# Layer 1 attention of a two-layer graph network: when the group ends, the transferred sums and the special tiles fall

## The chip, the cores and the metric

The kernel runs on one core of a Trainium2 chip. A core has five engines with queues of their own: TensorE (PE, matrix products; PEld is its loading of weights), VectorE (DVE), ScalarE (ACT), GpSimd (POOL) and SyncE (SP, which here only issues DMA transfers), and 16 DMA engines that all queues share. The metric is the device time of one execution in microseconds. The kernel before takes 2959.15 us, the median of three runs (2958.06 to 2962.82).

## The reference

`x` is 4096 x 512 and `adj` a 4096 x 4096 matrix of zeros and ones. Two residual layers follow each other, each on `h = relu(layernorm(x))`. Layer 0 is a masked attention by `h @ edge_w`. Layer 1, which the change concerns, is a graph attention with 8 heads of 64 columns:

```python
data1 = (h @ W.T + b).reshape(N, H, D)                 # N 4096, H 8, D 64
src = einsum('nhd,xhd->nh', data1, src_proj);  trg = einsum('nhd,xhd->nh', data1, trg_proj)
e = src.T[:, :, None] + trg.T[:, None, :]              # head, target n, source m
e = where(e >= 0, e, 0.01 * e) + adj[None]             # the mask is added as 0 or 1
out = einsum('hnm,hmd->hnd', softmax(e, axis=-1), data1.transpose(1, 0, 2))
x = x + out
```

`adj` is added and excludes nothing, so every head needs all 4096 x 4096 weights. A weight is exp(adj) times the larger of two products of a row factor and a column factor, since the exponential of a leaky relu of a sum is such a maximum. No exponential per head and pair is needed, only exponentials of `adj`, shared by the heads, and one multiply-by-maximum per head.

## The kernel before, in words

Layer 0 and the linear part of layer 1 fill the first 1729 us; nothing in them is changed. Then comes the loop of layer 1's attention. It has eight **groups**: four blocks of `WL` = 1024 target rows, each for two sets of four heads. A group has 32 **steps**, one per tile `m` of 128 source rows. One list of 256 steps runs through all groups, and `stages` at its end calls each stage so many steps ahead; the order of these calls is the order of every engine's queue, written by hand:

- `load` (3 steps ahead) puts the transfer of a 128 x 1024 tile of transposed `adj` into SP's queue (tile `e`, three buffers). At certain `m` it also fetches for the next group the row factors `z` of four heads and the row `u`.
- `exps` (1 ahead) writes exp(adj) to PSUM (`ex`, one buffer) on ACT; `last_exps` (2 ahead, in `factors`) writes a scaled exponential `e3` for head 3 of the set; `relus` (2 ahead) prepares head 0.
- `weigh` (1 ahead) makes the four products `pr3, pr0, pr1, pr2`, in that order, on DVE (lines 846 and 849), each 128 x 1024. `pr0` has three buffers, the others two. At a **special tile** (`BY_LOG`), `pr0` comes from ACT instead: `logs`, five steps ahead, makes a relu on ACT and starts a transfer on POOL that adds the `adj` tile to it; ACT later takes its exponential (line 832). DVE then has three products.
- `gather` (0 ahead) multiplies the products on PE with the values, in column tiles of 32, so that four matmuls run beside each other (line 881), and sums denominators in a fifth PSUM bank `dn` (line 886).

The denominator of heads 1 and 2 goes through PE in each step. For head 3, POOL adds the products `pr3` into one tile (`acc3`, lines 856 and 858). For head 0 the products of most tiles (`BY_DMA`) are added up by transfers that accumulate, into two tiles `acc00` and `acc01` in turn (lines 863 and 865); the other tiles go through PE with a column of ones, as a pair of matmuls. `by_pe` and `side` in `gather` alternate which half of the four column groups such a pair occupies. The last step of a group multiplies the collected sums with the ones column, and head 3's last product as well. ACT copies the results out of PSUM (`os`, line 910).

The end of a group runs inside the next group's steps: `finish` is a generator, and one `next(ending, None)` per step takes one part of it. It copies the denominators (ACT, line 916), turns them (PE, line 920), takes reciprocals (DVE, line 924), turns each of eight output tiles (two transposes, line 936), scales it (four small ACT copies, line 960), adds two at a time to the residual by a transfer of POOL (line 963), and stores them through SP (line 966). The last group has `finish_last` instead. Group 0 has the generator `tables`, which prepares `z` and `u`.

All waits between engines are semaphores that follow from who reads and writes which tile. A buffer that is written again waits for its last reader, transfers included.

Of the kernel before, what the change touches and what calls it, by code (L numbers as in the profile page):

```python
# [8 lines left out]
FP = mybir.dt.float32  # L9
AF = mybir.ActivationFunctionType  # L10
ALU = mybir.AluOpType
# [4 lines left out]
P = 128  # L16
# [12 lines left out]
def kernel(  # L29
# [15 lines left out]
    nc = tc.nc  # L45
# [675 lines left out]

    HV = WL // BL
    JT = BL // P
    Q = P // 4
    BY_LOG = (17, 21, 25, 29)
    BY_DMA = [m for m in range(2, NT - 5) if m % 4 != 1]

    with tc.tile_pool(name="p", bufs=2) as prp, tc.tile_pool(name="rl", bufs=2) as rlp, tc.tile_pool(
        name="io1", bufs=3
    ) as iop, tc.tile_pool(name="s1", bufs=1) as sp, tc.tile_pool(name="za", bufs=1) as zp0, tc.tile_pool(name="e3", bufs=2) as e3p, tc.tile_pool(
        name="zb", bufs=1
    ) as zp1, tc.tile_pool(name="e", bufs=3) as ep, tc.tile_pool(name="ac", bufs=2) as acp, tc.tile_pool(
        name="os", bufs=1
    ) as osp, tc.tile_pool(name="u", bufs=1) as usp, tc.tile_pool(
        name="p_x", bufs=1, space=PSUM
# [11 lines left out]
        def tables():  # L750

            for h in range(H):
                nc.scalar.activation(s_n[:, h, :], s_n[:, h, :], AF.Relu, bias=tmb[:, h:h + 1])
                if h % 3 == 2:
                    yield
            pz = p_t.tile([P, 2, P], FP, name="pt")
            for g in range(H // HG):
                nc.tensor.transpose(pz[:NT, g, :], s_n[:, g * HG, :], ident)
            yield
            ut = sp.tile([NT, 2, P], FP, name="ut")  # L760
            nc.scalar.copy(ut, pz[:NT])
            nc.gpsimd.dma_start(u_d.rearrange("g t p -> t g p"), ut)
            nc.scalar.activation(s_n, s_n, AF.Exp, scale=-(1.0 - SLOPE))
            yield
            s_f = s_n.rearrange("p h t -> p (h t)")
            for c in range(H * NT // P):
                pz = p_t.tile([P, P], FP, name="pt")
                nc.tensor.transpose(pz, s_f[:, c * P:(c + 1) * P], ident)
                yield
                zt = sp.tile([P, P], FP, name="zt", bufs=2)  # L770
                nc.scalar.copy(zt, pz)
                nc.gpsimd.dma_start(z_d[c * P:(c + 1) * P, :], zt)
            yield
# [12 lines left out]
        def load(i, m):  # L786
            b, g = groups[i]
            e = ep.tile([P, WL], FP, name="e")
            nc.sync.dma_start(e, adj_t[m * P:(m + 1) * P, b * WL:(b + 1) * WL])
            ra[i, m] = e  # L790
            if i + 1 < len(groups) and m == 28:
                us[i + 1] = usp.tile([P, WL], FP, name="u")
                b, g = groups[i + 1]
                nc.sync.dma_start(us[i + 1], row_bcast(u_d, WL, g * N + b * WL))
            if i + 1 < len(groups) and m in (20, 22, 24, 26):
                zload(i + 1, ORDER[(m - 20) // 2])

        def scale(i, m):

# [17 lines left out]
            nc.scalar.activation(x_, ra[i, m], AF.Exp, bias=ld_m[:, h // HG, m:m + 1])  # L817
            e3[i, m] = x_

        def logs(i, m):  # L820
            if m in BY_LOG:
                b, g = groups[i]
                r = rlp.tile([P, WL], FP, name="lg", bufs=1)
                nc.scalar.activation(r, us[i], AF.Relu, bias=nlg_m[:, g, m:m + 1], scale=-(1.0 - SLOPE))
                nc.gpsimd.dma_start(r, adj_t[m * P:(m + 1) * P, b * WL:(b + 1) * WL], accum_op=ALU.add)
                rl[i, m] = r
# [11 lines left out]
        def weigh(i, m, order=ORDER):  # L838
            h = groups[i][1] * HG
            x_ = ex.pop((i, m))  # L840
            for k in order:
                if (i, m, k) in pr:
                    continue
                w = prp.tile([P, WL], FP, name=f"pr{k}", bufs=3 if k == 0 else 2)
                if k == 0:
                    nc.vector.scalar_tensor_tensor(w, rl.pop((i, m)), ngd_m[:, h // HG, m:m + 1], x_,  # L846
                                                   op0=ALU.subtract, op1=ALU.mult)
                else:
                    nc.vector.scalar_tensor_tensor(w, zs_[i, k], g_m[:, h + k, m:m + 1],  # L849
                                                   e3.pop((i, m)) if k == 3 else x_,  # L850
                                                   op0=ALU.max, op1=ALU.mult)
                pr[i, m, k] = w
            w = pr[i, m, 3]
            if m == 1:
                acc[i, 3] = acp.tile([P, WL], FP, name="acc3", bufs=1)
                nc.gpsimd.tensor_tensor(acc[i, 3], pr[i, 0, 3], w, ALU.add)
            elif 1 < m < NT - 1:
                nc.gpsimd.tensor_tensor(acc[i, 3], acc[i, 3], w, ALU.add)  # L858
            if m in BY_DMA:
                n = BY_DMA.index(m)  # L860
                if n < 2:
                    acc[i, 0, n] = acp.tile([P, WL], FP, name=f"acc0{n}", bufs=1)
                    nc.gpsimd.dma_start(acc[i, 0, n], pr[i, m, 0])
                else:
                    nc.gpsimd.dma_start(acc[i, 0, n % 2], pr[i, m, 0], accum_op=ALU.add)

        def gather(i, m):
            b, g = groups[i]
# [26 lines left out]
                    den(side * HV + q, zo[:, 1 - side:3], pr[i, m, 0], q, start=False, stop=False)  # L895
            if last:
                for q in range(HV):
                    den(HV + q, zo[:, 1:3], pr[i, m, 3], q, start=False, stop=False)
                for q in range(HV):
                    den(q, zo[:, 1:3], acc[i, 0, 1], q, start=False, stop=False)  # L900
                for r, a in enumerate((acc[i, 0, 0], acc[i, 3])):
                    for q in range(HV):
                        den(r * HV + q, zo[:, 1:3], a, q, start=False, stop=True)
# [9 lines left out]
        def denominators(i):  # L913
            os_, dn = late.pop(i)
            od = osp.tile([P, BL], FP, name="od")
            nc.scalar.copy(od, dn)
            yield os_
            pd = p_t.tile([P, JT, 2, 4], FP, name="pt")
            for j in range(JT):
                nc.tensor.matmul(pd[:, j, :, :].rearrange("p e r -> p (e r)"), od[:, j * P:(j + 1) * P],  # L920
                                 pick.rearrange("p e r -> p (e r)"), start=True, stop=True)
            yield
            rd = sp.tile([P, JT, 2, 4], FP, name="rd")
            nc.vector.reciprocal(rd, pd)
            yield rd

# [18 lines left out]
        def finish(i):  # L945


            dens = denominators(i)
            os_ = next(dens)
            yield  # L950
            next(dens)
            yield
            rd = next(dens)
            pts, os2 = {}, {}
            for t in range(WT + 4):
                if 0 < t <= WT:
                    if t % 2:
                        o = iop.tile([P, 2, HG, D], FP, name="o")
                    for r, k in enumerate(ORDER):
                        nc.scalar.activation(o[:, (t - 1) % 2, k, :], pts[t - 1][:, r, :], AF.Copy,  # L960
                                             scale=share(rd, t - 1, r))
                    if t % 2 == 0:
                        nc.gpsimd.dma_start(o, part(x1, i, t - 2, 2), accum_op=ALU.add)
                        os2[t] = o
                if t - 3 in os2:
                    nc.sync.dma_start(part(out, i, t - 5, 2), os2[t - 3])
                if t < WT:
                    pts[t] = p_t.tile([P, HG, D], FP, name="pt")
                    turn(os_, t, pts[t])
                yield  # L970

        def finish_last(i):

# [5 lines left out]
            os_ = next(dens)  # L979
            pts = [p_v.tile([P, HG, D], FP, name=f"pv{c}{q}") for q in range(HV) for c in range(2)]  # L980
            xs = p_x.tile([P, 4, HG, D], FP, name="ex")
            pts += [xs[:, n, :, :] for n in range(4)]
            for t in range(4):
                turn(os_, t, pts[t])
            next(dens)
# [28 lines left out]
        for k in ORDER:  # L1014
            zs_[0, k] = zp0.tile([P, WL], FP, name=f"z{k}")
            nc.sync.dma_start(zs_[0, k], row_bcast(s_d, WL, k * WL))
        load(0, 1)
        load(0, 2)
        first_e = ra[0, 0]
        exps(0, 0)  # L1020
        ra[0, 0] = first_e
# [28 lines left out]
        factors(0, 1)  # L1050
        scale(0, 1)

        stages = ((load, 3), (logs, 5), (exps, 1), (weigh, 1), (factors, 2), (scale, 2), (gather, 0))
        for s in range(len(steps)):
            for f, ahead in stages:
                if s + ahead < len(steps):
                    f(*steps[s + ahead])
            if s == 0:
                ending = tables()
            elif s % NT == 0:  # L1060
                ending = finish(s // NT - 1)
            if s == len(steps) - 2:
                ending = finish_last(len(groups) - 1)
            next(ending, None)
        for _ in ending:
            pass

# [33 lines left out]
```

## Time and profile before

| what | us |
|---|---|
| median of three runs | 2959.15 (2958.06 to 2962.82) |
| the profiled execution, its own time | 2957.07 |
| its span, first to last instruction | 2955.3 |
| the attention loop, from its first line 881 | 1729.4 on |
| group 0, with the loop's start | 155.25 |
| groups 1, 2, 3 | 150.74, 151.04, 152.38 |
| groups 4, 5, 6 | 150.21, 152.10, 150.22 |
| group 7, to the first transpose of the tail | 151.99 |

The profiled execution has 1.8 us outside its span. A group is measured from PE's first line 881 in it to that of the next group. PE's granted clock is 0.995 of full speed. In the attention loop the engines show 151.3 us (PE), 148.8 (DVE), 119.7 (ACT) and 94.8 (POOL) of busy time per group; the DMA engines have a mean share of 0.77 to 0.85. Products on DVE overlap: each is shown with 1.27 us, while their starts lie 1.19 us apart.

### The profile page before, as it was taken

Reading aid. Unit: us, or ns where it says so; the run is one execution under the profiler, and the core shown is the slowest. Engines: PE = TensorE matmul, PEld = TensorE weight load, DVE = VectorE, ACT = ScalarE, POOL = GpSimd, SP = SyncE. Lnnn points to the kernel's source line nnn. Section 1 sums busy time; section 2 is a strip of 40 time slices with the busy share of each in tenths; the row PEclk is TensorE's granted clock in tenths of the full one; section 3 lists DMA queues with packets and bytes.
Section 4 is the critical chain, followed back from the end, with each engine's and each line's share of the span. In section 5 each row is a group of like instructions: output and inputs, shape, how many; then the busy total and the mean of one; then the engine's idle time right before and its main releaser. Section 6 shows DMA issues by size and latency. Waiting matters only on the chain.

```text
span 2955.3 us, 42955 instructions
## 1 busy us (share of the span) xinstructions
PE 2911.4 (99%) x15179; PEld 1137.7 (38%) x15179; DVE 2534.6 (86%) x3584; ACT 1325.5 (45%) x1822; POOL 1380.0 (47%) x1043
## 2 busy tenths in 40 slices
PE   8999999999999999999999989999999999999998
PEld 4444444444444444444444423323222322232222
DVE  5435777778888998998996789999999999999998
ACT  2211111111121221221221068888777777777776
POOL 3401111113444444444444756565757575757574
PEclk9999999999999999999999999999999999999999
DMA  5525666667876766756653259696969696979795
GB/s 181 172 78 200 223 218 225 226 218 187 205 178 162 177 161 187 186 166 180 190 167 127 61 152 242 187 258 188 256 191 249 194 250 204 243 202 243 208 232 153
DMA packets 485160, 570.89 MB, mean 193 GB/s; under 512 B 265080, under 2 KB 315288, under 8 KB 484944
## 3 DMA queue, kind: packets, MB, share of 16 engines
q1 hardware_dynamic: 431920, 406.70, 45.8%
q0 software_dynamic: 51008, 157.51, 23.2%
q10 hardware_dynamic: 2016, 3.93, 0.4%
q8 instruction: 119, 1.95, 0.3%
q14 instruction: 97, 0.79, 0.1%
HBM read 415.76 MB, written 72.55 MB: 165 GB/s over the span
## 4 chain that ended last, share of the span: by engine, by line
PE 92%; DVE 4%; ACT 2%; DMA 1%; issue 1%; SPq 0%; POOL 0%; DVEq 0%; ACTq 0%; POOLq 0%
PE po L480 29%; PE pv L881 27%; PE pe L331 15%; PE dn L886 9%; PE po L591 4%; PE ps L196 3%; PE pe L203 3%; DVE pr L849 2%; PE pt L936 1%; ACT e L817 1%; DMA acc<-pr 1%; DMA xt<-in_x_dram 0%; DVE acc_z L154 0%; DVE pt L441 0%; PE pt L920 0%
## 5 line engine op out<-in xcount | busy, mean ns | idle before, releaser
L881 PE MATMUL pv<-pr,sup 128*32 128x512 f32 x8192 | 1010.0, 594 | 9.0 <-POOL d_m L1046 5.4
L480 PE MATMUL po<-sup,at 128*128 128x512 f32 x2048 | 887.2, 594 | 3.8 <-DVE at L450 3.8
L858 POOL TENSOR_TENSOR acc<-acc,pr 128x1024 f32<-128x1024 f32 x232 | 558.2, 2406 | 318.1 <-DVE pr L849 317.8
L849 DVE SCALAR_TENSOR_TENSOR pr<-z,g_m,ex 128x1024 f32<-128x1024 f32 x512 | 631.0, 1273 | 5.2 <-ACT ex L807 4.1
L480 PEld LDWEIGHTS po<-sup,at 128*128 128x128 f32 x2048 | 387.1, 190 | 483.2 <-issue 446.3
L460 POOL TENSOR_TENSOR racc<-racc,ex 128x512 f32<-128x512 f32 x240 | 362.3, 1510 | 385.3 <-ACT ex L444 383.8
L881 PEld LDWEIGHTS pv<-pr,sup 128*32 128x32 f32 x8192 | 286.7, 110 | 593.2 <-issue 533.6
L444 ACT ACTIVATE ex<-d 128x512 f32<-128x512 f32 x256 | 160.5, 630 | 624.7 <-DVE d L442 616.5
L331 PE MATMUL pe<-he_t,he_t 128*128 128x512 f32 x896 | 386.4, 592 | 0.0
L807 ACT ACTIVATE ex<-e 128x1024 f32<-128x1024 f32 x256 | 263.0, 1027 | 227.2 <-DVE pr L849 226.6
L849 DVE SCALAR_TENSOR_TENSOR pr<-z,g_m,e 128x1024 f32<-128x1024 f32 x256 | 328.9, 1285 | 9.9 <-PE pv L881 5.9
L886 PE MATMUL dn<-pr,d_m 128*2 128x512 f32 x1984 | 335.6, 592 | 0.0
L817 ACT ACTIVATE e<-e,ld_m 128x1024 f32<-128x1024 f32 x256 | 291.0, 1137 | 6.5 <-DMA e<-in_adj_t_dram 6.3
L846 DVE SCALAR_TENSOR_TENSOR pr<-rl,ngd_m,ex 128x1024 f32<-128x1024 f32 x224 | 285.0, 1273 | 1.6 <-ACT ex L807 1.2
L835 ACT ACTIVATE rl<-z,ngd_m,d_m 128x1024 f32<-128x1024 f32 x224 | 275.0, 1228 | 0.0
L450 DVE TENSOR_TENSOR at<-ex,a 128x512 f32<-128x512 f32 x256 | 189.5, 740 | 71.1 <-ACT ex L444 48.0
L331 PEld LDWEIGHTS pe<-he_t,he_t 128*128 128x128 f32 x896 | 169.2, 190 | 210.1 <-issue 190.5
L335 POOL DMA_DIRECT2D e_d<-es x144 | 78.4, 545 | 364.8 <-ACT es L334 359.2
L334 ACT COPY es<-pe 128x512 f32<-128x512 f32 (+2 forms) x144 | 79.1, 550 | 377.2 <-PE pe L331 377.2
L442 DVE TENSOR_TENSOR d<-pt,mk 128x512 f32<-128x512 f32 x256 | 177.0, 691 | 8.8
L336 DVE CUSTOM_DVE_ANT_0 mk<-pe,mk 128x512 f32<-128x512 f32 (+2 forms) x144 | 93.0, 645 | 98.9 <-ACT es L334 98.8
L435 DVE TENSOR_SCALAR mk<-a 128x512 f32<-128x512 f32 x256 | 128.5, 502 | 2.2 <-DMA a<-in_adj_t_dram 2.2
(186 smaller groups left out, 2564.9 us busy)
## 6 DMA issues: line engine op xcount, KB each, us to landing
e<-in_adj_t_dram SPq DMA_DIRECT2D x256, 512.0 KB, 5.5
acc<-pr POOLq DMA_DIRECT2D x152, 512.0 KB, 5.7
a<-in_adj_t_dram SPq DMA_DIRECT2D x256, 256.0 KB, 3.8
ar<-in_adj_dram SPq DMA_DIRECT2D x120, 256.0 KB, 3.0
e_d<-es POOLq DMA_DIRECT2D x120, 256.0 KB, 3.1
eb<-e_d SPq DMA_DIRECT2D x456, 64.0 KB, 3.0
ac<-in_adj_t_dram SPq DMA_DIRECT2D x112, 256.0 KB, 3.5
et<-e_d SPq DMA_DIRECT2D x112, 256.0 KB, 3.8
```

The lines of the kernel that those rows point to most:

```text
L331: nc.tensor.matmul(pe[:, :w], he_t[i][:, k, (t % TB) * P:(t % TB + 1) * P], he_t[j][:, k, BL - w:], start=(k == 0), stop=(k == KC - 1))
L450: nc.vector.tensor_tensor(w, e, aj.pop((b, m)), ALU.mult)
L460: nc.gpsimd.tensor_tensor(racc, racc, e, ALU.add)
L480: nc.tensor.matmul(po[j], w[:, j * P:(j + 1) * P], sup[:, m, :], start=(m == 0), stop=last)
L807: nc.scalar.activation(x_, ra.pop((i, m)), AF.Exp)
L817: nc.scalar.activation(x_, ra[i, m], AF.Exp, bias=ld_m[:, h // HG, m:m + 1])
L835: nc.scalar.activation(r, zs_[i, 0], AF.Relu, bias=ngd_m[:, h // HG, m:m + 1], scale=d_m[:, h, m:m + 1])
L846: nc.vector.scalar_tensor_tensor(w, rl.pop((i, m)), ngd_m[:, h // HG, m:m + 1], x_, op0=ALU.subtract, op1=ALU.mult)
L849: nc.vector.scalar_tensor_tensor(w, zs_[i, k], g_m[:, h + k, m:m + 1], e3.pop((i, m)) if k == 3 else x_, op0=ALU.max, op1=ALU.mult)
L858: nc.gpsimd.tensor_tensor(acc[i, 3], acc[i, 3], w, ALU.add)
L881: nc.tensor.matmul(v[c][q][r * D + c0:r * D + c0 + Q, :], va[:, m, g * HG + k, c0:c0 + Q], pr[i, m, k][:, q * BL:(q + 1) * BL], start=(m = ...
L886: nc.tensor.matmul(dn[r * Q:r * Q + w.shape[1], :], w, src[:, q * BL:(q + 1) * BL], **fl)
```

## The change

It touches the attention loop alone. Steps are counted from 0 within a group.

- **Buffers.** Tile `e` gets four buffers (three before) and is loaded four steps ahead (three); the output tile `o` two (three), `zt` three (two), `rd` two (one).
- **Group end.** `finish` turns two output tiles at a time (four transposes into one PSUM tile), then scales them in the two following parts. It has 15 parts, and `PARTS` says in which steps one is taken: 0 to 4, 6 to 8, 11 to 13, 18 to 20 and 22, instead of every step from 0 on.
- **Sums by transfer.** `BY_DMA` has 22 tiles (19 before), tiles 0 and 1 among them; the first two transfers, plain copies, both start with tile 1. Ten tiles are left to PE (thirteen). The last product of head 3 is added by POOL like the others, and its own pair of matmuls in the last step goes.
- **Special tiles** are 9, 16, 21 and 27 (17, 21, 25, 29), with the relu in steps 2, 10, 15 and 22, placed after the exponentials and factors of that step instead of before them.
- **Loads for the next group.** From group 1 on, the four `z` rows are fetched two by two with `e` tiles 3 and 4, thus around the group's start; in group 0 with tiles 22 and 23. Before, one each with tiles 20, 22, 24 and 26.
- **Small.** The first three `adj` tiles after tile 0 are loaded at the start (two before); the tail's output tiles alternate between two PSUM banks in another order.

```diff
-    BY_LOG = (17, 21, 25, 29)
-    BY_DMA = [m for m in range(2, NT - 5) if m % 4 != 1]
+    PARTS = (0, 1, 2, 3, 4, 6, 7, 8, 11, 12, 13, 18, 19, 20, 22)
+    BY_LOG = {9: 2, 16: 10, 21: 15, 27: 22}
+    BY_DMA = [m for m in range(NT) if m not in (4, 8, 13, 14, 19, 23, 24, 25, 29, 31)]
...
-        name="io1", bufs=3
+        name="io1", bufs=2
...
-    ) as zp1, tc.tile_pool(name="e", bufs=3) as ep, tc.tile_pool(name="ac", bufs=2) as acp, tc.tile_pool(
+    ) as zp1, tc.tile_pool(name="e", bufs=4) as ep, tc.tile_pool(name="ac", bufs=2) as acp, tc.tile_pool(
...
-            if i + 1 < len(groups) and m in (20, 22, 24, 26):
-                zload(i + 1, ORDER[(m - 20) // 2])
+            m0 = 3 if i else 22
+            if i + 1 < len(groups) and m0 <= m < m0 + 2:
+                for k in ORDER[2 * (m - m0):2 * (m - m0) + 2]:
+                    zload(i + 1, k)
...
-        def logs(i, m):
-            if m in BY_LOG:
+        def logs(i, s):
+            for m in [m for m in BY_LOG if BY_LOG[m] == s]:
...
-            elif 1 < m < NT - 1:
+            elif m > 1:
                 nc.gpsimd.tensor_tensor(acc[i, 3], acc[i, 3], w, ALU.add)
-            if m in BY_DMA:
-                n = BY_DMA.index(m)
-                if n < 2:
+            if m == 1:
+                for n in range(2):
                     acc[i, 0, n] = acp.tile([P, WL], FP, name=f"acc0{n}", bufs=1)
-                    nc.gpsimd.dma_start(acc[i, 0, n], pr[i, m, 0])
-                else:
-                    nc.gpsimd.dma_start(acc[i, 0, n % 2], pr[i, m, 0], accum_op=ALU.add)
+                    nc.gpsimd.dma_start(acc[i, 0, n], pr[i, n, 0])
+            elif m > 1 and m in BY_DMA:
+                nc.gpsimd.dma_start(acc[i, 0, BY_DMA.index(m) % 2], pr[i, m, 0], accum_op=ALU.add)
...
             if last:
-                for q in range(HV):
-                    den(HV + q, zo[:, 1:3], pr[i, m, 3], q, start=False, stop=False)
                 for q in range(HV):
                     den(q, zo[:, 1:3], acc[i, 0, 1], q, start=False, stop=False)
...
-            pts, os2 = {}, {}
-            for t in range(WT + 4):
-                if 0 < t <= WT:
-                    if t % 2:
-                        o = iop.tile([P, 2, HG, D], FP, name="o")
-                    for r, k in enumerate(ORDER):
-                        nc.scalar.activation(o[:, (t - 1) % 2, k, :], pts[t - 1][:, r, :], AF.Copy,
-                                             scale=share(rd, t - 1, r))
-                    if t % 2 == 0:
-                        nc.gpsimd.dma_start(o, part(x1, i, t - 2, 2), accum_op=ALU.add)
-                        os2[t] = o
-                if t - 3 in os2:
-                    nc.sync.dma_start(part(out, i, t - 5, 2), os2[t - 3])
-                if t < WT:
-                    pts[t] = p_t.tile([P, HG, D], FP, name="pt")
-                    turn(os_, t, pts[t])
+            old = None
+            for t in range(0, WT, 2):
+                pt = p_t.tile([P, 2, HG, D], FP, name="pt")
+                for j in range(2):
+                    turn(os_, t + j, pt[:, j, :, :])
+                yield
+                o = iop.tile([P, 2, HG, D], FP, name="o")
+                for j in range(2):
+                    for r, k in enumerate(ORDER):
+                        nc.scalar.activation(o[:, j, k, :], pt[:, j, r, :], AF.Copy, scale=share(rd, t + j, r))
+                    if j == 0:
+                        if t:
+                            nc.sync.dma_start(part(out, i, t - 2, 2), old)
+                        yield
+                nc.gpsimd.dma_start(o, part(x1, i, t, 2), accum_op=ALU.add)
+                old = o
                 yield
+            nc.sync.dma_start(part(out, i, WT - 2, 2), old)
+            yield
...
-            pts += [xs[:, n, :, :] for n in range(4)]
+            pts += [xs[:, n, :, :] for n in (0, 2, 1, 3)]
...
-        load(0, 1)
-        load(0, 2)
+        for m in range(1, 4):
+            load(0, m)
...
-        stages = ((load, 3), (logs, 5), (exps, 1), (weigh, 1), (factors, 2), (scale, 2), (gather, 0))
+        stages = ((load, 4), (exps, 1), (weigh, 1), (factors, 2), (logs, 0), (scale, 2), (gather, 0))
...
-            next(ending, None)
+            if s < NT or s % NT in PARTS or s > len(steps) - 3:
+                next(ending, None)
```

More of the change, by code (lines that the diff above doesn't have):

```diff
@@ L769, in tables @@
                 yield
-                zt = sp.tile([P, P], FP, name="zt", bufs=2)
+                zt = sp.tile([P, P], FP, name="zt", bufs=3)
                 nc.scalar.copy(zt, pz)
@@ L922, in denominators @@
             yield
-            rd = sp.tile([P, JT, 2, 4], FP, name="rd")
+            rd = sp.tile([P, JT, 2, 4], FP, name="rd", bufs=2)
             nc.vector.reciprocal(rd, pd)
```

## The prediction

> **What bounds the kernel now.** I read the page first, then busy time by stretch (once by group, once by step), then the timelines around a group's end, then waits and landings. The page's totals and its 40 slices:
>
> ```profile
> PE 2911.4 (99%) x15179; PEld 1137.7 (38%) x15179; DVE 2534.6 (86%) x3584; ACT 1325.5 (45%) x1822; POOL 1380.0 (47%) x1043
> PE   8999999999999999999999989999999999999998
> DVE  5435777778888998998996789999999999999998
> ```
>
> TensorE (PE) is full everywhere, but in the last 17 slices, layer 1, VectorE (DVE) is full too: two engines share the bound there, and 86% hides it. The busy time of two whole groups (groups 4 and 5; columns: stretch, length, PE, PEld, DVE, ACT, POOL, clock, DMA share, GB/s) tells which is ahead:
>
> ```profile
> 2338.80:2489.01 150.21, 150.21 (x1374) 43.90 (x1368) 148.63 (x126) 117.08 (x139) 95.24 (x57) 1.00 0.84 225
> 2489.01:2641.11 152.10, 152.09 (x1381) 44.92 (x1378) 148.96 (x126) 116.60 (x137) 95.16 (x57) 1.00 0.84 222
> ```
>
> PE sets the length; DVE's own work is only some 1.6 us shorter. Groups 1 to 6 take 906.7 us, mean 151.1; groups 1 to 7 with the last PE step 1058.7. Steps of group 4 (4, 5, 12, 17, 31), and one of group 3 (28):
>
> ```profile
> 2358.93:2363.73 4.80, 4.80 (x43) 1.35 (x42) 4.80 (x5) 4.06 (x8) 3.65 (x3) 1.00 0.68 177
> 2363.73:2369.37 5.64, 5.64 (x47) 1.53 (x46) 5.64 (x5) 4.91 (x9) 4.09 (x3) 1.00 0.90 209
> 2398.02:2402.31 4.29, 4.29 (x45) 1.25 (x40) 4.29 (x5) 2.75 (x4) 2.14 (x1) 1.00 1.04 216
> 2419.49:2424.63 5.14, 5.14 (x53) 1.48 (x49) 5.14 (x5) 3.55 (x4) 3.21 (x2) 1.00 1.00 277
> ...
> 2482.99:2489.01 6.02, 6.02 (x62) 1.63 (x56) 5.22 (x5) 6.02 (x9) 0.00 (x0) 1.00 0.29 90
> ...
> 2317.72:2322.50 4.78, 4.51 (x46) 1.16 (x42) 4.78 (x5) 3.78 (x4) 2.40 (x2) 1.00 0.44 129
> ```
>
> A bare step is 4.29 us of PE; turning one output tile adds 0.51 (4.80); a round of ones-columns matmuls adds 0.85 (5.14); step 5 has both (5.64). DVE needs 4 products x 1.19 us (their starts lie 1.19 apart, though each shows 1.27) = 4.77, or 3.58 at a special tile. So PE is slower than DVE in steps 1 to 9, where every group end is crowded, and faster in the bare steps after. DVE runs ahead until the pr tiles are full, then waits for PE (0.4 to 0.7 us around steps 6 and 10). By step 25 the lead is used up, and in groups 3 and 5 PE starves: 4.78 in a bare step is DVE's pace.
>
> **What the Trainium skill says.** "TensorEngine Tiling (Array Packing)", Key Properties: column tiles run independently, and changing the tiling mode drains the engine. The trace agrees: a turn costs 0.51, while eight transposes in a row at the kernel's end take 1.02, or 0.13 each. Two of 0.13 leave 0.25 for going to the full array and back. "DMA: Bandwidth & Descriptors", SWDGE vs HWDGE vs iDMA: accumulation during a transfer is GpSimd's (POOL's) alone, so every added sum joins POOL's one queue; here too all are issued there. Its fit (Anatomy of one DMA) of 2.0 us + bytes / 436e3 gives 3.2 us for 512 KB, as an estimate; plain copies here land in 2.9 to 4.7, accumulating ones in 4.6 to 10.0, so the trace's numbers are used.
>
> **The change, part by part, per group.**
>
> *Ones-columns matmuls.* Tiles summed by PE fall from 13 to 10, and the last step's own pair for head 3 goes (that product now joins POOL's sum). A pair fills half of the four column groups (one "side"), and sides alternate, so two pairs make one round unless a full-array operation drains between them. Before: 7 + 6 tiles and 2 + 2 pairs at the end, 9 against 8: nine rounds, and a tenth because turns stand between tiles 5 and 9. The trace shows ten: steps 5, 9, 17, 25, 28, 30; two in step 31; two around the next step 1. Bare steps 32 x 4.29 + eight turns 4.08 + ten rounds 8.5 + denominators' transposes 1.1 = 151.0, as measured. After: 5 + 5, and 2 + 1 at the end: seven rounds, and one more because step 6's turn stands between tiles 4 and 8. Two rounds fewer: -1.7.
>
> *Turns.* Eight turns of two transposes become four of four: 8 x 0.51 = 4.1 becomes 4 x (0.25 + 4 x 0.13) = 3.1, so -1.0 (-0.3 if a transpose amid tiled work costs 0.18; taken: -1.0). PE is then 151.0 - 2.7 = 148.3.
>
> *DVE.* Products and reciprocal stay: 148.6 of work. It also waits on ScalarE (ACT): 4.1 us in all for the exponentials (mostly special tiles held back by a full pr0) and 3.7 at group ends, 7.8 / 8 = 1.0 per group. The first falls: of the new special tiles only 9 and 21 follow, three tiles on, a transferred sum (all four did), and the z loads no longer stretch those sums. The second about halves, as pr3 is no longer read by PE's last pairs. I take 0.55. DVE is 149.2, now above PE.
>
> *Spread of the group end.* With extra PE work over steps 1 to 31 and special tiles at 9, 16, 21, 27, I follow the lead (DVE's start of a step ahead of PE's, by the timelines) from the 4.9 us that step 1 of group 3 has (2190.74 - 2185.86), adding PE's step and taking away DVE's: it stays between about 4.5 and 7.3, under the 8.3 at which DVE was blocked and over the 2.3 to 2.8 at which PE starved. So neither blocks the other, and a group costs the larger sum, 149.2.
>
> *Group 0* has no turns and is paced by DVE. Only its end shortens: one round less after the last product (-0.85); tables and the first special relu now meet in step 2, ACT 5.1 us against 4.77 (+0.3). About -0.6.
>
> *Costed at nothing.* The special relu (1.04) moves behind exponentials 0.96 + 1.04 and relu 1.13: 4.2 of ACT in 4.77, and it stands in steps without output copies (2, 10, 15, 22); in a copying step 3.1 + 0.9 fits as well; without that cover it costs DVE 0.4 each. Behind it on POOL stands its own transfer (0.94 issue, 9.5 to land), still 3 to 5 steps before use. POOL per step: add 2.35 (starts apart) + issue 0.6 to 0.9, and 1.25 for an output tile: at most 4.5 of 4.77. SP's queue: the z loads go two per step behind the e loads of steps 3 and 4; their old tiles are free by then, and a fourth e buffer gives one step (4.77) more against their 9.7. An output store waits for its transfer (16 such waits, 2.8 at most) with e loads behind it; the same buffer covers that. The tail's PSUM order lets ACT and DVE overlap: 0 to -1.4 by their waits there; I take -0.5.
>
> *Three more sums per group.* About 2.4 us of all 16 engines each, 7 us on a share of 0.84 x 151 = 127: some 0.90 of 149. The z loads leave the crowded steps 17 to 23, where the share is 1.05. What is tight is new: the first two sums both start after tile 1's add.
>
> ```profile
> 2187.62 2.39 POOL L856 TENSOR_TENSOR acc<-pr,pr 128x1024 f32<-128x1024 f32 x1 [12.84 <-PE dn L886]
> 2196.60 1.28 DVE L846 SCALAR_TENSOR_TENSOR pr<-rl,ngd_m,ex 128x1024 f32<-128x1024 f32 x1
> ```
>
> ```profile
> DMA to landing us min/median/max: 2.9/3.0/4.7
> DMA to landing us min/median/max: 4.6/5.9/10.0
> ```
>
> Above, from the timelines, the first line is POOL's add at the start of group 3, held until PE has read the old sum; the second, DVE writing pr0 of tile 3, the third buffer on, which after the change must find sum 0 landed. From 2190.0 to 2196.6 are 6.6 us; the plain copies of L863 (the upper of the two lines of landings) land in 3 to 5; the accumulating ones of L865 (the lower) need up to 10 under z loads, and z loads now precede these by about 10 us. I take no stall; bounds 0 and 3 us per group.
>
> Sum: groups 1 to 7, 1058.7 - 7 x 149.2 = -14.3; group 0 -0.6; tail -0.5: -15.4. The profiled execution took 2957.07 (span 2955.3), giving 2941.7. Runs have a median 2.1 above it: 2943.8, say **2944**.
>
> **Rivals.**
> 1. *DVE binds harder.* ACT's waits stay at 1.0 or grow to 1.5 per group: 149.6 to 150.1, 0.4 to 0.9 in each of seven groups: 2947 to 2950. For: groups 3 and 5 lost 1.3 to 1.6 at one special tile. Against: those were behind z loads.
> 2. *Collision at the group's start.* Sum 0 lands 2 us late; DVE's tile 3 is late, its reciprocal behind it, and PE's first turn waits for that. 7 x 2 = 14 against 15 gained: 2957, no change.
> 3. *Slower.* The same place, if the first sums take 10 us: 3.4 late in each of seven groups, +24, 2968. It decides from 9.6 us of landing: (2965.1 - 2943.8) / 7 = 3.0 late. For: 10.0 occurs. Against: the z loads have mostly landed, and with only e loads under way transfers land in 3.0.
> 4. *The matmul saving does not come* because drains fall elsewhere (one round instead of two): PE 149.1, hidden under DVE's 149.2, so nothing is lost; if the turns save only 0.3 as well, PE is 149.9 and binds, 0.7 x 7 = 5 more: 2949.
>
> **How the numbers follow.** Forecast 0.58 (2939 to 2948), rivals 1 and 4 together 0.20, rival 2 0.12, rival 3 and the like 0.10. About 0.2%, 5.9 us, is what a measurement can tell: faster is under 2953.2. That is 0.58 + 0.17 of the 0.20 + 0.01: 0.76 faster; same 0.14; slower 0.10. The range 2937 to 2957 leaves out a little of the first case, half of rival 2 and all of rival 3.
>
> **What would show it.** Right: groups of about 149, even from 1 to 7; four turns per group; eight rounds; POOL's adds 248; no starved bare step at 25 to 28; DVE gaps under 0.6 per group. Wrong: DVE waiting for a transfer at tile 3, a turn in step 2 waiting for the reciprocal, sums landing past 9 us, or ACT's exponential of tiles 9 or 21 waiting for a sum.

## The result and the profile after

The changed kernel takes 2952.4 us, the median of ten runs (2948.5 to 2955.3), against 2958.1 before; the ratio is 0.9982, with a 95% interval of 0.9974 to 0.9989. It is faster, by 0.18% where 0.5% was forecast: the gain of 15 us came to 6. The profiled execution has a span of 2949.9 us (2955.3 before).

The page's totals of the changed kernel, and its chain of work that ended last by engine:

```profile
PE 2895.0 (98%) x15051; PEld 1152.0 (39%) x15051; DVE 2535.0 (86%) x3584; ACT 1318.9 (45%) x1822; POOL 1421.7 (48%) x1075
PE 74%; DVE 12%; ACT 7%; issue 4%; DMA 3%; POOL 0%; SPq 0%; DVEq 0%; ACTq 0%; POOLq 0%
```

PE lost 16 us of busy time and no longer fills the chain of work that ended last: ACT, DVE and transfers have a larger part in it (before, PE had 92% of it, DVE 4%, ACT 2%, transfers 1%). Busy time by group, for groups 4, 5 and 6 (columns as before: stretch, length, PE, PEld, DVE, ACT, POOL):

```profile
2335.83:2486.13 150.30, 148.90 (x1360) 45.79 (x1356) 148.67 (x126) 115.59 (x138) 99.89 (x61) 1.00 0.91 235
2486.13:2636.15 150.02, 148.82 (x1361) 50.15 (x1357) 148.66 (x126) 115.63 (x138) 99.98 (x61) 1.00 0.92 236
2636.15:2787.75 151.60, 149.48 (x1360) 43.59 (x1356) 148.67 (x126) 115.66 (x138) 99.94 (x61) 1.00 0.89 227
```

PE is no longer busy for the whole length of a group, and its busy time includes matmuls drawn out while they wait (step 23 below). DVE's work is the same 148.7 in these three, and the length is that plus DVE's waits for ACT (1.6, 1.4 and 2.9 us). Groups 1 to 7 take 151.70, 149.80, 150.98, 150.30, 150.02, 151.60 and 150.19, mean 150.66 (before 151.24, forecast 149.2). Group 0 takes 155.76 (before 155.25, forecast -0.6), the tail 11.96 (before 11.98). The rest of the span's difference, 1.8 us, lies ahead of the loop, where the runs below differ as much: their loops start at 1726.6 to 1729.2.

Three steps of group 4 (6, 18 and 23), by stretch:

```profile
2364.64:2370.46 5.82, 5.82 (x52) 1.73 (x45) 5.82 (x6) 3.58 (x4) 3.64 (x3) 1.00 1.04 255
2420.12:2425.11 4.99, 4.99 (x48) 1.54 (x41) 4.99 (x5) 3.23 (x3) 3.11 (x2) 1.00 1.05 263
2442.60:2447.45 4.85, 4.85 (x48) 2.04 (x44) 4.85 (x5) 4.35 (x5) 3.35 (x3) 1.00 0.97 225
```

A turn of two tiles costs 4.99 - 4.29 = 0.70, and 0.68 in step 6 beside the round of tile 4; the forecast was 0.77. Step 23 has only a bare step's work, 4.29, and is a starved one: PE follows DVE there, as in steps 22 and 30 (4.58 and 4.70). In steps 26 to 28 of this group PE keeps its 4.29.

In the changed kernel the lines that matter are: on ACT `exps` 812, `last_exps` 822, `relus` 840, the special tile's relu 829 and exponential 837, the output copies 965; on DVE the products 851 (head 0) and 854; on POOL the special tile's transfer 830 and the sums 869. `weigh` runs one step ahead, so tile 9's products are made in step 8.

What DVE waits for in groups 1 to 7, before (the first three lines) and after (the last two): who, for whom, us in total, times, longest:

```profile
DVE pr L849 <- PE pv L881: 7.0, 13, 0.7
DVE pr L849 <- ACT os L910: 3.7, 7, 0.8
DVE pr L849 <- ACT ex L807: 3.7, 4, 1.6
```

```profile
DVE pr L851 <- ACT ex L812: 9.5, 28, 0.9
DVE pr L854 <- ACT ex L812: 3.7, 5, 1.8
```

The waits for ACT rose from 7.4 to 13.2 us in seven groups, where 3.9 (0.55 a group) had been forecast. The waits for PE, 7.0 before, are gone. Line 851 is the product for head 0, the first that needs exp(adj), and it waits four times in every group. By DVE's timeline the 13.2 are 1.8 at tile 1, 1.9 at tile 10, 3.4 at tile 17, 3.7 at tile 21 and 2.3 at tile 22. Two of the places, in ACT's timeline of group 4, with DVE's lines after:

```profile
2375.84 1.13 ACT L822 ACTIVATE e<-e,ld_m 128x1024 f32<-128x1024 f32 x1
2376.89 1.23 ACT L840 ACTIVATE rl<-z,ngd_m,d_m 128x1024 f32<-128x1024 f32 x1
2378.03 0.89 ACT L965 ACTIVATE o<-pt,rd 128x64 f32<-128x64 f32 x4
2378.81 1.03 ACT L812 ACTIVATE ex<-e 128x1024 f32<-128x1024 f32 x1
...
2410.56 1.13 ACT L829 ACTIVATE lg<-u,nlg_m 128x1024 f32<-128x1024 f32 x1
2411.60 1.01 ACT L812 ACTIVATE ex<-e 128x1024 f32<-128x1024 f32 x1
```

```profile
2375.95 2.47 DVE L854 SCALAR_TENSOR_TENSOR pr<-z,g_m,ex 128x1024 f32<-128x1024 f32 x2
2378.34 1.33 DVE L854 SCALAR_TENSOR_TENSOR pr<-z,g_m,e 128x1024 f32<-128x1024 f32 x1
2379.87 1.28 DVE L851 SCALAR_TENSOR_TENSOR pr<-rl,ngd_m,ex 128x1024 f32<-128x1024 f32 x1 [0.21 <-ACT ex L812]
...
2412.64 1.28 DVE L851 SCALAR_TENSOR_TENSOR pr<-rl,ngd_m,ex 128x1024 f32<-128x1024 f32 x1 [0.43 <-ACT ex L812]
```

At 2375.95 DVE makes the last two products of special tile 9. It has made only three in that step, so it is ready for tile 10 after 3.58 us instead of 4.77. ACT has the step's usual 3.13 us of work and behind it four output copies (0.78); the exponential of tile 10 starts at 2378.81 right behind these, without a pause, and DVE waits 0.21. After special tile 16 the same happens with the relu of special tile 21, queued in that step: DVE waits 0.43 at tile 17. Group 1 has the small `scale` operations as well, and both waits are longer there, 0.70 and 0.90; group 0, which has no copies, has only the second, 0.90. Tile 21 has a second trouble, the transfer that must free its buffer:

```profile
2429.43 1.15 ACT L837 ACTIVATE pr<-lg,t_m 128x1024 f32<-128x1024 f32 x1 [1.46 <-DMA acc<-pr]
2430.49 0.91 ACT L965 ACTIVATE o<-pt,rd 128x64 f32<-128x64 f32 x4
2431.28 1.04 ACT L812 ACTIVATE ex<-e 128x1024 f32<-128x1024 f32 x1
```

ACT waits 1.46 us for sum 18, then has copies, and the next exponential comes 0.54 us late for DVE; in group 6 this is 1.84. Tile 22 then waits 0.26 behind the copies of step 20.

What stands ahead of sum 18 in POOL's queue, in the same group:

```profile
2411.99 0.86 POOL L830 DMA_DIRECT2D lg<-in_adj_t_dram  x1
2414.91 1.20 POOL L869 DMA_DIRECT2D acc<-pr  x1
2420.00 0.85 POOL L869 DMA_DIRECT2D acc<-pr  x1
```

Sums 15 and 16 have landed after 4.7 and 4.9 us. The special tile's own transfer follows (9.8 us to landing), directly behind it sum 17 (10.5) and then sum 18 (9.3).

### The profile page after: what moved, and what is told of

It reads as the page before. It is cut to its first block, busy times and chain, and to the rows that moved or that the text cites. A ratio compares the mean times of both kernels' runs of the same rounds, so it can differ in the third digit from the quotient of the medians.

```text
span 2949.9 us, 42840 instructions
## 1 busy us (share of the span) xinstructions
PE 2895.0 (98%) x15051; PEld 1152.0 (39%) x15051; DVE 2535.0 (86%) x3584; ACT 1318.9 (45%) x1822; POOL 1421.7 (48%) x1075
## 4 chain that ended last, share of the span: by engine, by line
PE 74%; DVE 12%; ACT 7%; issue 4%; DMA 3%; POOL 0%; SPq 0%; DVEq 0%; ACTq 0%; POOLq 0%
PE po L480 29%; PE pe L331 15%; PE pv L885 14%; DVE pr L854 9%; PE dn L890 4%; PE po L591 4%; PE ps L196 3%; ACT e L822 3%; PE pe L203 3%; DMA acc<-pr 1%; ACT rl L840 1%; ACT ex L812 1%; DVE pr L851 1%; DMA e<-in_adj_t_dram 0%; PE pt L938 0%
## 5 line engine op out<-in xcount | busy, mean ns | idle before, releaser
L885 PE MATMUL pv<-pr,sup 128*32 128x512 f32 x8192 | 1024.0, 595 | 13.2 <-POOL d_m L1050 5.4
L863 POOL TENSOR_TENSOR acc<-acc,pr 128x1024 f32<-128x1024 f32 x240 | 583.7, 2432 | 328.6 <-DVE pr L854 326.7
L885 PEld LDWEIGHTS pv<-pr,sup 128*32 128x32 f32 x8192 | 301.9, 110 | 604.6 <-issue 503.4
L890 PE MATMUL dn<-pr,d_m 128*2 128x512 f32 x1984 | 347.6, 592 | 0.0
L869 POOL DMA_DIRECT2D acc<-pr x160 | 150.0, 937 | 1.2 <-DMA acc<-pr 0.5
```

Source lines behind the costliest of these rows:

```text
L885: nc.tensor.matmul(v[c][q][r * D + c0:r * D + c0 + Q, :], va[:, m, g * HG + k, c0:c0 + Q], pr[i, m, k][:, q * BL:(q + 1) * BL], start=(m = ...
L890: nc.tensor.matmul(dn[r * Q:r * Q + w.shape[1], :], w, src[:, q * BL:(q + 1) * BL], **fl)
```

## The experiments

Theory A: DVE is the bound of the changed kernel, and ACT holds it up where relu or copies are queued in a three-product step, and at tile 21. Rival B: PE is the bound by new waits at a group's start, where it waited 6.7 us in seven groups for the copy of the denominators. Rival C: transfers are saturated. All ratios are to the kernel before, which took 2957.0 to 2958.1 beside these runs; a difference to the changed kernel is therefore good to about 1 us, apart from the spread of the runs.

**The relu ahead of the exponentials again.**

```diff
-        stages = ((load, 4), (exps, 1), (weigh, 1), (factors, 2), (logs, 0), (scale, 2), (gather, 0))
+        stages = ((load, 4), (logs, 0), (exps, 1), (weigh, 1), (factors, 2), (scale, 2), (gather, 0))
```

> The changed kernel with one thing undone: the special tiles' relu stands before a step's exponentials again, in the same steps 2, 10, 15 and 22. Theory A (VectorE is the bound, and ScalarE holds it up in the 3.58 us that it takes for a special tile, when relu or copies are queued there): the wait after tile 16 goes, 0.43 us in groups 2 to 7 and 0.9 in groups 0 and 1, sum 4.4; the time falls from 2952.4 to about 2948. Rival B (TensorE is the bound, by its new waits in steps 0 to 2 for the copy of the denominators and the reciprocal): no change. Rival C (the transfers are saturated, and only the waits for sums count): no change.

Measured 2949.8 us, ratio 0.9973 (0.9964 to 0.9983). DVE's wait after tile 16 is gone from the trace. The gain in time is 2.5 us for a forecast 4.4, with an interval that parts it neither from 4.4 nor from nothing, so this run alone shows the wait's cause and not its worth. The waits at tile 21 stayed, at 5.1 us over all groups.

**No copies in a three-product step.**

```diff
-    PARTS = (0, 1, 2, 3, 4, 6, 7, 8, 11, 12, 13, 18, 19, 20, 22)
+    PARTS = (0, 1, 2, 3, 4, 6, 7, 9, 11, 12, 13, 18, 19, 21, 23)
```

> The changed kernel with the group end's parts of steps 8, 20 and 22 taken in steps 9, 21 and 23, so that no output copies stand in the steps in which VectorE makes the three products of tiles 9 and 21. Theory A: the waits at tiles 10 and 22 go, 0.21 + 0.26 us in groups 2 to 7 and 0.70 + 0.73 in group 1, sum 4.2; about 2948. Rivals B and C: no change.

Measured 2947.9 us, ratio 0.9970 (0.9958 to 0.9981), 4.5 less than the changed kernel, where A has 4.2; the two intervals still touch. The waits at tiles 10 and 22 are gone from every group.

**Special tile 22 for 21.**

```diff
-    BY_LOG = {9: 2, 16: 10, 21: 15, 27: 22}
+    BY_LOG = {9: 2, 16: 10, 22: 15, 27: 22}
```

> The changed kernel with special tile 22 in place of 21, so that its buffer is freed by TensorE (tile 19) and not by a transferred sum (tile 18), and its three-product step holds no copies. Theory A: both the wait for the sum (0.06 to 1.84 us a group, 4.7 in all eight) and the wait for the copies behind it (2.3) go; 7 us less, about 2945. Rival C: 4.7 less, 2948. Rival B: no change.

Measured 2942.9 us, ratio 0.9952 (0.9938 to 0.9966): 9.5 less, against A's 7. Only the waits at tiles 1, 10 and 17 are left in groups 1 to 7, and the lengths of groups 4 to 7 now lie within 0.15 us.

**All collisions removed.**

```diff
-    PARTS = (0, 1, 2, 3, 4, 6, 7, 8, 11, 12, 13, 18, 19, 20, 22)
-    BY_LOG = {9: 2, 16: 10, 21: 15, 27: 22}
+    PARTS = (0, 1, 2, 3, 4, 6, 7, 9, 11, 12, 13, 18, 19, 20, 22)
+    BY_LOG = {9: 2, 16: 10, 22: 16, 27: 22}
```

> The changed kernel with special tile 22 for 21, its relu in step 16 instead of 15, and the part of step 8 in step 9: no relu and no copies are left in any three-product step, and only special tile 9 follows a transferred sum. Theory A: the waits of VectorE for ScalarE fall from 2.0 to about 0.2 us per group, groups take 148.9 to 149.2, and the time is 13 us less at most, 2940 to 2943, as first forecast. Rival B: 2950 to 2952, with TensorE's waits in steps 0 to 2 unchanged. Rival C: about 2948.

Measured 2936.7 us, ratio 0.9932 (0.9918 to 0.9945): 15.7 less than the changed kernel, more than A's 13. The whole of DVE's waits in groups 1 to 7 of this run (tile 1 alone), and one of its groups by stretch:

```profile
DVE pr L851 <- ACT ex L812: 1.8, 7, 0.7
```

```profile
2328.45:2476.96 148.51, 148.44 (x1362) 44.07 (x1359) 148.33 (x126) 115.91 (x138) 99.78 (x61) 1.00 0.93 238
```

13.2 has become 1.8, and PE and DVE are both full. Transfers are as many as in the changed kernel and PE's work is the same, so B and C fall as the main cause. B's own sign goes too: nothing at the group's start was edited, and PE's waits there for the copy of the denominators fall from 6.7 us to 1.7. A few moved entries in ACT's order, and one buffer freed by PE instead of a transfer, bring the time 21 us under the kernel before, where 15 had been forecast for the change itself.

**PE's ones-columns matmuls left out**, in the changed kernel and in the one before (this leaves out ten or thirteen tiles' part of a denominator, so the output is not the reference's).

```diff
-            if m in by_pe:
+            if m in by_pe and m < 0:
```

> The changed kernel without the ten pairs of ones-columns matmuls that TensorE does per group: it leaves out those ten tiles' part of one head's denominator in each set of four. TensorE loses eight rounds but those of the last step, 5 to 6 us per group. Theory A (VectorE and its waits for ScalarE are the bound of the changed kernel): groups stay at 150 to 151.7 and the time falls by 0 to 4 us, to 2948 to 2952. Rival B (TensorE is the bound): 8 x 5 = 40 us less, 2912.

> The kernel before without its thirteen pairs of ones-columns matmuls per group: it leaves out those thirteen tiles' part of one head's denominator in each set of four. TensorE loses about 6.8 us per group, 151.0 to 144. If TensorE was the bound before, as the prediction has it, the time falls until VectorE binds at 148.6 of work and about 1.0 of waits: groups 149.6, 1.6 us each less, 2947 to 2948. If VectorE was the bound before as well, no change; if TensorE alone counts, 50 us less.

The changed kernel without them takes 2952.4 us, ratio 0.9984 (0.9978 to 0.9991): nothing for about 5 us of PE work per group, with DVE's waits at 12.3 in groups 1 to 7. The kernel before falls to 2946.9, ratio 0.9966 (0.9952 to 0.9979), as expected, to groups of 149.0 to 151.8. Group 4 of each, the changed kernel first:

```profile
2335.88:2485.91 150.03, 147.25 (x1318) 45.84 (x1316) 148.66 (x126) 115.55 (x138) 99.91 (x61) 1.00 0.92 236
2332.35:2481.54 149.19, 147.16 (x1327) 46.60 (x1320) 148.58 (x126) 116.85 (x138) 95.25 (x57) 1.00 0.84 226
```

So PE was the bound before and is not after: shown from both sides. And with PE's excess away the old special tiles ran at 2946.9, 5.5 us less than the changed kernel: in the traces 3.4 in groups 1 to 7, where DVE waits 9.9 against 13.2, and 2.3 in group 0.

**The old special tiles in the changed kernel**, with the relu ahead of the exponentials.

```diff
-    BY_LOG = {9: 2, 16: 10, 21: 15, 27: 22}
+    BY_LOG = {17: 12, 21: 16, 25: 20, 29: 24}
-        stages = ((load, 4), (exps, 1), (weigh, 1), (factors, 2), (logs, 0), (scale, 2), (gather, 0))
+        stages = ((load, 4), (logs, 0), (exps, 1), (weigh, 1), (factors, 2), (scale, 2), (gather, 0))
```

> The changed kernel with its special tiles undone: 17, 21, 25 and 29 as before, relu in steps 12, 16, 20 and 24 ahead of the exponentials, everything else as changed. By theory A the waits of VectorE per group are 0.2 at the start, 0.26 behind the copies of step 20, some 0.3 where the relu of step 20 follows the copies of step 19, and those for sums 18 and 22 that tiles 21 and 25 need (0.5 and 0.2): 1.4 against the 2.0 of the changed kernel, so 4 us less than that, 2948. If the move of the special tiles was what helped (spread of the load), it is slower than the changed kernel instead, 2955 or more, with bare steps of 4.77 late in a group.

Measured 2965.2 us, ratio 1.0030 (1.0018 to 1.0043). The expectation of 2948 missed by 17. The first experiment has the same order and differs from this one in the special tiles alone, and it is 15.4 us faster: the move of the special tiles did help. The time thus fits the other sentence of the expectation, but the trace shows another cause than a spread load: one place, tile 21, costs 2.2 to 3.2 us in each group, 22.0 in all against 5.1 in the first experiment. ACT's timeline in group 3, then DVE's:

```profile
2286.50 1.15 ACT L837 ACTIVATE pr<-lg,t_m 128x1024 f32<-128x1024 f32 x1 [2.09 <-DMA acc<-pr]
2287.56 0.91 ACT L965 ACTIVATE o<-pt,rd 128x64 f32<-128x64 f32 x4
2288.34 1.16 ACT L829 ACTIVATE lg<-u,nlg_m 128x1024 f32<-128x1024 f32 x1
2289.38 1.04 ACT L812 ACTIVATE ex<-e 128x1024 f32<-128x1024 f32 x1
```

```profile
2290.45 2.47 DVE L854 SCALAR_TENSOR_TENSOR pr<-z,g_m,ex 128x1024 f32<-128x1024 f32 x2 [2.21 <-ACT ex L812]
```

A wait for sum 18 of 2.1, copies of 0.8 and the relu of 1.04 stand in a row ahead of the exponential. With the relu behind the exponential, as in the changed kernel, only the first two would; no run has the old special tiles in that order, so what it is worth here is not shown. The order hurts after tile 16 in any case: what counts is which step the relu falls in. The 0.5 that I had taken for sum 18 was what DVE lost to it in the changed kernel (0.54 in group 4), where ACT's own wait was already 1.46; here ACT waits 2.09, and the copies and the relu behind that wait leave DVE no cover, so it loses 2.21.

**Why sum 18 is late.** Tile 17 summed by PE, 19 by transfer.

```diff
-    BY_DMA = [m for m in range(NT) if m not in (4, 8, 13, 14, 19, 23, 24, 25, 29, 31)]
+    BY_DMA = [m for m in range(NT) if m not in (4, 8, 13, 14, 17, 23, 24, 25, 29, 31)]
```

> The changed kernel with tile 17 summed by TensorE and tile 19 by transfer, so that sums 15, 16 and 18 stand before special tile 21, with a step without a transfer between them, instead of 15 to 18 without a break. If the four transfers in a row are what makes sum 18 land late (8.3 to 10.4 us after issue in the changed kernel, 5.1 to 8.7 before), it lands within about 7.7 us here, ScalarE's wait for it before tile 21 goes, VectorE's wait there (0.06 to 1.84 us a group, 4.7 in all) as well, and the time is 2947 to 2949; the extra round that TensorE pays, as the turn of step 18 now follows an odd pair, is hidden. If the special tile's own transfer, started one step before, is what holds it up, sum 18 still lands after 9 us and the time stays at 2952.

Measured 2948.2 us, ratio 0.9970 (0.9958 to 0.9982). The landing of sum 18 in group 4, in the changed kernel (the first) and here:

```profile
DMA to landing us min/median/max: 9.3/9.3/9.3
```

```profile
DMA to landing us min/median/max: 4.9/4.9/4.9
```

In groups 1 to 7 it lands in 4.9 to 6.0 us instead of 8.3 to 10.4, and the wait at tile 21 is gone there. Only in group 0, where the z loads fall on this place, it takes 10.2 and DVE waits 1.0. So the special tile's transfer does not make sum 18 late when a step without a sum follows it.

That four stand in a row is not the cause, though. The run with all collisions removed has the same four, but issues the special tile's transfer behind sum 17 instead of ahead of it; POOL's lines in its group 4, sum 17 first:

```profile
2406.98 0.86 POOL L869 DMA_DIRECT2D acc<-pr  x1
2407.86 0.87 POOL L830 DMA_DIRECT2D lg<-in_adj_t_dram  x1
2411.74 0.87 POOL L869 DMA_DIRECT2D acc<-pr  x1
```

Here sum 17, the third of the row, lands after 5.8 us (5.8 to 7.3 in all groups, against 10.1 to 11.7 in the changed kernel), and sum 18 after 9.9. In the first experiment that transfer stands ahead of sum 16, and sum 16 takes 9.1 to 9.9. In each of these runs the late sum is the one directly behind the special tile's transfer, and the next stay late while every step adds one. To that extent rival C was right, at one place.

**A fifth special tile.**

```diff
-    BY_LOG = {9: 2, 16: 10, 21: 15, 27: 22}
+    BY_LOG = {7: 1, 11: 5, 16: 11, 22: 16, 27: 22}
```

> The changed kernel with five special tiles, 7, 11, 16, 22 and 27, with their relu in steps 1, 5, 11, 16 and 22; none of their three-product steps (6, 10, 15, 21, 26) holds a relu or copies, and only tile 22's, 16's, 11's, 7's and 27's third predecessors (19, 13, 8, 4, 24) are TensorE's, so none waits for a sum. VectorE's work falls by 1.19 to 147.4 per group. By theory A TensorE is then the bound: 148.0 of work and what is left of its wait for the copy of the denominators, 148.0 to 148.5 per group, 2933 to 2937. If more transfers (one of 512 KB more per group) hurt, DVE waits for sums and it is 2940 or more.

Measured 2936.2 us, ratio 0.9926 (0.9912 to 0.9939), not to be told from the run with all collisions removed. A group of it by stretch:

```profile
2329.13:2477.31 148.18, 148.18 (x1362) 44.45 (x1359) 147.53 (x125) 117.06 (x140) 100.63 (x62) 1.00 0.94 241
```

DVE has slack now and is stopped by PE; groups 2 to 5 are 148.18 each. This is PE's own length after the change.

## Why the prediction was right or wrong

- *What bounds the kernel before* was right: without its ones-columns matmuls it falls by 10 us to DVE's pace and DVE's waits, as worked out.
- *Ones-columns matmuls and turns, PE 148.3*: right. Where PE alone binds, a group is 148.18; turns cost 0.70 for a forecast 0.77. (The prediction's aside, -0.3 if a transpose costs 0.18, gives -0.6 by its own figures: 8 x 0.51 - 4 x 0.87. Nothing hangs on it.)
- *DVE, 148.6 of work*: right (148.6 to 148.7 in groups 1 to 6, but 149.1 in group 3).
- *DVE waits 0.55 per group*: this is the step that failed. It was 13.2 / 7 = 1.9. The part at the group's start came as forecast (0.19 a group, with 0.66 in group 1); the rest has two lines of the working behind it. "Costed at nothing" set ACT's work (4.2 with a relu, 4.0 with copies) against a step of 4.77. But steps 8, 15 and 20 are those of special tiles, in which DVE takes 3.58; ACT has no cover there. The price that I had named for a missing cover, 0.4, is what the relu cost after tile 16 (0.43). These steps make 7.7 of the 13.2 us. And "the z loads no longer stretch those sums" was true from group 1 on, but not enough: the special tile's own transfer was set at nothing because it lands in time for its use, but sums 17 and 18 stand behind it in POOL's queue. Sum 18 landed after 8.3 to 10.4 us and held tile 21 up in five of seven groups, 3.7 us.
- *The sum*: seven groups at 150.66 instead of 149.2 are 10.2 us, and group 0 at +0.5 instead of -0.6 is 1.1. With the tail's missing 0.5, and less the 1.8 gained ahead of the loop, that is the missing gain of 10 in the profiled executions. In group 0 the relu beside the tables cost 0.2, and the relu after tile 16 and tile 21 together 1.65.
- *Spread of the group end*: the lead did not stay above 4.5. In group 4 it lies between 3.7 and 5.8 up to step 20 and at 2.3 to 3.1 from step 23 on, and PE starved in steps 22, 23 and 30, since DVE was the slower by more than I had counted. With the waits removed PE no longer waits for DVE in groups 1 to 7.
- *Rivals*: the first, DVE binding harder, is what happened, through two causes it did not name and beyond its 1.5. The collision at the group's start did not come: plain copies landed in 3.0 to 5.6, and no product waited for sum 0. The saving of matmuls, which the fourth doubted, did come.
- *Three more sums per group*: the 2.4 us of the DMA engines for each had no figure beside it. By group 4's share and length, 0.84 of 150.2 before and 0.91 of 150.3 after, it is about 3.5 (an estimate), and the share came to 0.91 to 0.92 instead of 0.90. It is what stands directly ahead of a sum that cost time, not the share.
- *The tail's order* of PSUM banks saved nothing: the waits of 0.7 us between ACT and DVE are still there.

## What to carry to other kernels

Where two engines bound a loop together, check the helper engine's queue against the shortest step of its consumer, not the mean one: a step that was made cheap for one engine has the least room for another's extra work. Where a buffer is freed by a transfer, look at what stands directly ahead of that transfer in its queue, and whether a free step follows. And a change that lightens one of two bounds is worth only what the other one leaves, its waits included.

## What the runs showed of the hardware

Equal accumulating transfers of 512 KB land after times that differ by a factor of two, by what was issued just before. In group 4 sum 18 took 4.9 us after a step without a sum. Sums 17 and 18 took 10.5 and 9.3 close behind the special tile's transfer, while sums 15 and 16 ahead of it took 4.7 and 4.9. The share of the DMA engines over the group is 0.91 to 0.92 both times, and in group 4 of the changed kernel POOL's transfers land in the order in which they were issued. And two more transposes behind the first two cost PE only 0.19 us (0.70 against 0.51), less than the 0.26 counted from the row of eight.
